# Row additions moved to TensorE, a merged scan, weights loaded in pieces and a later softplus in a Mamba block kernel

## The chip, the core and the metric

The kernel runs on one core of one Trainium2 chip. A core has five engines that run their own instruction streams in order: TensorE (PE, matrix products, with a separate row PEld for loading the stationary operand), VectorE (DVE), ScalarE (ACT), GpSimd (POOL) and SyncE (SP, which here only issues DMA transfers). The metric is the device time of one execution in microseconds (us), taken as the median of several runs. Times inside an execution come from one profiled execution and count from the start of its span.

## What is computed

The input is a tensor of 4 batches by 1024 rows by 256 columns, in fp32. The block has two halves, each around a residual sum:

```python
x = x + attn(layernorm(x))
x = x + ffn(layernorm(x))

# attn(h): a Mamba layer and a gated MLP
h = h + mamba(rmsnorm(h))
h = h + silu(rmsnorm(h) @ gate.T) * (rmsnorm(h) @ up.T) @ down.T

# mamba(u): z, x, B, C, dt_raw = split(u @ in_proj.T)
dt = softplus(dt_raw @ dt_proj.T + bias)
state = exp(dt * A) * state + (dt * x) * B      # for each of 1024 rows, one after the other
y = sum over 32 states of state * C
out = (y + x * D) * silu(z) @ out_proj.T

# ffn(x): hidden of 1024
out = fwht(silu(x @ W1.T) * (x @ W3.T)) @ W2.T
```

The state has 256 channels times 32 states for each batch, so the recurrence is 8192 independent scans over 1024 rows per batch. This scan is the heart of the kernel. The Hadamard transform (fwht) is folded into W2 at the start of the kernel (`w2h`).

## The kernel before

**Units, quarters and ticks.** The work is cut into eight units: four batches, each in two chunks of 512 rows (c = 0 and c = 1, in this order). A chunk with c = 0 starts with a zero state; its last states are kept in `carry` and are the start of the scans of the c = 1 chunk. The 8192 scans of a unit are cut into 16 groups called q, each a tile `da` of 128 partitions by 4 by 512. A group takes two ticks, each of which handles two of the four 512-column tiles. So a unit has 32 ticks, t0 to t31 in the text, and there are 128 groups in all.

**One tick of the scan** has these steps. DMA has brought dt, repeated over partitions, into `da` (`dma_da`, L753 is the common helper `spread`, from the DRAM tile `dtd`), dt times x into `ub` (`dma_ub`, from the DRAM tile `ud`), and C into `cr`. ACT turns `da` into exp(A * dt) for two tiles, two ticks ahead of their use (`exp`, L791). DVE multiplies `ub` by B (`times_b`, L819: `bx` = `ub` * `pb`, 1024 columns in PSUM, where `pb` is a copy of B made once in 16 ticks by `copy_b`, L808), and then runs two scans of 512 columns, in place in `da` (`scan`, L828). After a group POOL multiplies all 2048 columns by C (`times_c`, L841) and PE sums over states by a selecting matmul into the PSUM tile `py` (`sum_states`, L852; the first of eight groups also adds x * D by the diagonal `dd`, L850). There are five `da` buffers and four `ub` buffers.

**Around the scan** two functions put the dense work of other units into the same ticks. `pre(u, H)` makes the inputs of a unit before its first tick H: normalisation, projections, softplus (`act_dt`, L440), and the writes of dt, dt * x, B and C to DRAM. `post(u, E)` does the rest of a unit after its last tick, E being the first tick of the next unit: `y` (L870) copies `py` to `yt`; out_proj with weights `wo`; RMS norm; gate and up (`wg`, `wu`); down (`wd`); layer norm; W1 and W3; and W2 (`w2h`), which runs in the unit after that. So in a unit of the steady state, t3 has out_proj of the unit before, t5 to t8 W2 of the unit before that, t11 to t16 gate and up, t19 to t22 down, t27 to t34 W1 and W3. `many` is true for the first six units, whose `post` is spread over a whole unit.

**Adding to the residual rows.** `hr` holds the rows of a unit's normalised input; out_proj, down and W2 are added to it. `add_rows` issues the matmuls for four row tiles of 128 (L322) and has three ways to add. Way "pe": one more matmul of the identity with `hr` (L320) starts the accumulation in PSUM, and ACT (`replace`, L336) copies the sum back into `hr`. Way "pool": ACT copies the product from PSUM (`evict`, L344), and POOL adds it one tick later (L348). No way: DVE adds straight from PSUM (L332). Down uses "pe"; out_proj of the first six units and W2 of the first seven use "pool". `hr` itself is made by ACT from x (`scaled_rows`, L210) in t3 and t4 of the next unit.

**The order** is written by hand. `at(tick, lane, fn)` puts a step into a lane of a tick, and a loop runs the lanes of each tick in a fixed order: PE, ACT, `times_b`, ACTb (there `copy_b`), the exponentials, the first scan, DVE, the second scan, POOL0, `times_c`, POOL, `sum_states`, PEend, ACTend, SP, `dma_ub` for the tick four later, `dma_da` for the group three later, `dma_cr`, SPend. The `yt` copy is put into ACTend of the tick t2 while the loop is running, behind what stands there already. Each engine executes its instructions in this order; SP issues the DMAs in it, and a transfer whose source or buffer is not free holds up those behind it on SP. In unit 0, the weights `had`, `wd`, `w1` and `w3` are loaded by SP at ticks 5, 9, 15 and 21.

The lines that the steps of the prediction name: L320 and L322 the matmuls of `add_rows`, L332, L336, L344 and L348 its ways to add, L440 softplus, L791 exp, L808 the copy of B, L819 bx, L828 the scan, L841 the product with C, L850 and L852 the sums, L870 the `yt` copy, L236 projections (`project`), L280 `up` and L284 `product` of `gated`, L210 `scaled_rows`.

Of the kernel before, what the change touches and what calls it, by code (L numbers as in the profile page):

```python
# [9 lines left out]
F32 = mybir.dt.float32  # L10
AF = mybir.ActivationFunctionType
ALU = mybir.AluOpType
# [3 lines left out]
P = 128  # L16
BATCH, SEQ, DM = 4, 1024, 256
DFF = 704
HID = 1024
T = 512  # L20
# [7 lines left out]
def tile_block(ctx: ExitStack, tc: tile.TileContext, a, out):  # L28
# [20 lines left out]
    nc = tc.nc  # L49

    wp = ctx.enter_context(tc.tile_pool(name="w", bufs=1))
    p1 = ctx.enter_context(tc.tile_pool(name="p1", bufs=1))
# [5 lines left out]
    dr = ctx.enter_context(tc.tile_pool(name="dr", bufs=2, space=DRAM))  # L58
# [7 lines left out]
        return ps_m.tile([P, T], F32, tag="dense", name="dense")  # L66


    def load(name, shape, src, queue=nc.sync):
        t = wp.tile(shape, F32, tag=name, name=name)  # L70
        queue.dma_start(out=t, in_=src)
        return t
# [32 lines left out]
    W = {}  # L105
# [1 line left out]
    def load_k(name, cols, queue=nc.sync):  # L107
        W[name] = load(name, [P, 2, cols], a[name].rearrange("(k p) f -> p k f", p=P), queue)

    def load_wd():  # L110
        wd = W["wd"] = wp.tile([P, 6, DM], F32, tag="wd", name="wd")
        nc.sync.dma_start(
            out=wd[:, 0:5, :], in_=a["wd"][0:640, :].rearrange("(k p) f -> p k f", p=P)
        )
        nc.sync.dma_start(out=wd[0:64, 5, :], in_=a["wd"][640:DFF, :])

    def load_first():

# [129 lines left out]
    def at(tick, lane, fn, *args):  # L248
        todo[tick][lane].append(partial(fn, *args))

    def run(tick, lane):
        for fn in todo[tick].pop(lane, ()):
            fn()
# [109 lines left out]
    def pre(u, H):  # L363

        s = {}
# [69 lines left out]
        def act_dt(h):  # L435
            if h == 0:
                s["dt"] = [p2.tile([P, T], F32, tag="dt", name="dt") for _ in range(2)]
                u["dtd"] = dr.tile([2, 32, 4, T], F32, tag="dtd", name="dtd")
                u["ud"] = dr.tile([2, 32, 4, T], F32, tag="ud", name="ud")
            nc.scalar.activation(s["dt"][h], s["pv"][h], AF.Softplus, bias=dtb[:, h : h + 1])  # L440

        def dma_dt(h):
            nc.sync.dma_start(out=u["dtd"][h].rearrange("m b t -> b m t"), in_=s["dt"][h])

        def make_u(h, eng):
            s["du"] = p1.tile([P, T], F32, tag="du", name="du")
# [160 lines left out]
        for b in range(4):  # L607
            at(H - 19 + b, "SPend", dma_xr, 0, (b,))
            at(H - 14 + b, "SPend", dma_xr, 1, (b,))
        at(H - 15, "PE", pe_dt)  # L610
        at(H - 15, "PE", pe_c, 0)
        if H == 32:
            for h in range(2):
                at(H - 11, "PE", pe_z, h)
                at(H - 11, "ACTend", act_z, h)
        at(H - 15, "ACT", act_dt, 0)
        at(H - 15, "ACT", act_dt, 1)
        at(H - 14, "ACT", act_c, 0)
        at(H - 13, "POOL", make_u, 0, nc.gpsimd)
        at(H - 13, "SPend", dma_dt, 0)  # L620
        at(H - 11, "SPend", dma_c, 0)
        at(H - 11, "SPend", dma_u, 0)
        at(H - 10, "PE", pe_c, 1)
        at(H - 9, "ACT", act_c, 1)
        at(H - 1, "SPend", dma_c, 1)
# [5 lines left out]
    def post(u, E, other):  # L631


        s = {}
        last = u is us[-1]

        many = us.index(u) < len(us) - 2
# [34 lines left out]
        def store(lo=0, n=TT):  # L672
# [3 lines left out]
                in_=u["hr"][:, lo : lo + n, :],  # L676
            )

        at(E + 3, "ACT", hr, (0, 1))
        at(E + 4, "ACT", hr, (2, 3))  # L680
        add_rows(
            (E + 3,) * TT,
            u,
            lambda: [u["yt"][:, k, :] for k in range(2)],
            lambda: [W["wo"][:, k, :] for k in range(2)],
            "PEend",
            way="pool" if many else None,
        )
        for i in range(2):
            at(E + (5 + i if many else 4), "ACTend", row_stats, u, "hr", (2 * i, 2 * i + 1), False)  # L690
# [10 lines left out]
        for i in range(2):  # L701
# [8 lines left out]
            way="pe",  # L710
# [14 lines left out]
        for i in range(3):  # L725
# [5 lines left out]
            u,  # L731
            lambda: u["g"],
            lambda: [w2h[:, c, :] for c in range(8)],
            way=None if last else "pool",
        )
        if last:
            at(o2[1] + 1, "SPend", store, 0, 2)
# [20 lines left out]
    def dma_da(q):  # L758
        s = qs[q]
        s["da"] = pda.tile([P, 4, T], F32, tag="da", name="da")  # L760
        for b in (0, 2):
            spread(s, s["da"][:, b : b + 2, :], "dtd", b, 2)

    def dma_ub(q, half):
        s = qs[q]
        s["ub", half] = pub.tile([P, 2, T], F32, tag="ub", name="ub")
        spread(s, s["ub", half], "ud", 2 * half, 2)
# [18 lines left out]
    def exp(q, b):  # L786
        s = qs[q]
        if q == 0 and b == 0:
            s["da"] = pda.tile([P, 4, T], F32, tag="da", name="da")
        da = s["da"][:, b, :]  # L790
        nc.scalar.activation(  # L791
            da,
            da if q else s["u"]["pdt", b],
            AF.Exp,
            scale=an[:, s["h"], s["j"], b, s["g"] : s["g"] + 1],
        )

    def carry_of(s):
        return s["u"]["carry"][:, s["h"], s["j"], :, s["g"]]
# [10 lines left out]
    def times_b(q, b0):  # L810
        s = qs[q]
        u = s["u"]
        if q == 0:
            s["bx"] = ps_x.tile([P, 2, T], F32, tag="bx", name="bx")
            for i in range(2):
                nc.vector.tensor_tensor(s["bx"][:, i, :], u["pu", b0 + i], u["br", 0], ALU.mult)
            return
        s["bx"] = ps_x.tile([P, 2, T], F32, tag="bx", name="bx")
        nc.vector.tensor_tensor(  # L819
            s["bx"], s["ub", b0 // 2], u["pb"].unsqueeze(1).broadcast_to([P, 2, T]), ALU.mult  # L820
        )

    def scan(q, b):
        s = qs[q]
        u = s["u"]
        da = s["da"][:, b, :]
        start = 0.0 if u["c"] == 0 else carry_of(s)[:, b : b + 1]
        nc.vector.tensor_tensor_scan(da, da, s["bx"][:, b % 2, :], start, ALU.mult, ALU.add)  # L828

    def times_c(q, parts=(slice(0, 4),), eng=nc.gpsimd):  # L830
        s = qs[q]
        u = s["u"]
        if u["c"] == 0:
            if s["n"] == 0:
                kept = p2.tile([P, 2, 4, 4, 2], F32, tag="carry", name="carry")
                u["carry"] = us[us.index(u) + 1]["carry"] = kept
            nc.gpsimd.tensor_copy(carry_of(s), s["da"][:, :, T - 1])
        for part in parts:
            da = s["da"][:, part, :]
            n = da.shape[1]  # L840
            eng.tensor_tensor(da, da, s["cr"].unsqueeze(1).broadcast_to([P, n, T]), ALU.mult)  # L841

    def sum_states(q):
        s = qs[q]
        u = s["u"]
        first, last = s["n"] % 8 == 0, s["n"] % 8 == 7
        if first:
            u["py"] = ps_y.tile([P, T], F32, tag="y", name="py")
            x = u["xr"][:, s["h"], :]
            nc.tensor.matmul(u["py"], lhsT=dd[:, s["h"], :], rhs=x, start=True, stop=False)  # L850
        for b in range(4):
            nc.tensor.matmul(  # L852
                u["py"][32 * b : 32 * b + 32, :],
                lhsT=rsel[:, 2 * s["j"] + s["g"], :],
                rhs=s["da"][:, b, :],
                start=False,
                stop=last,
            )
        if last:
            if q == NQ - 1:  # L860
                at(2 * q + 4, "DVE", y_z_last, u)
            else:
                at(2 * q + 4, "ACTend", y, u, s["h"])
                at(2 * q + 5, "POOL0", y_z, u, s["h"])
# [14 lines left out]
    for k, u in enumerate(us):  # L879
        pre(u, 32 * k)  # L880
# [5 lines left out]
        nc.vector.tensor_scalar(nega, nega, -1.0, None, ALU.mult)  # L886

    at(-20, "PE", wake_pe)
    at(-18, "ACTend", load_first)
    at(-17, "ACTend", weights_ready)  # L890
    for h in range(2):
# [4 lines left out]
    at(-1, "SPend", dma_cr, 1)  # L896
    loads = [
        (5, load_had),
        (9, load_wd),
        (15, load_k, "w1", HID),  # L900
        (21, load_k, "w3", HID),
    ]
    for t, *f in loads:
        at(t, "SPend", *f)
# [11 lines left out]
    def has(q):  # L916
        return 0 <= q < NQ

    tick = min(todo)
    while todo:  # L920
        q, half = divmod(tick, 2)
        run(tick, "PE")
        run(tick, "ACT")
        if has(q) and tick:
            times_b(q, 2 * half)
        run(tick, "ACTb")
        if has(q + 1):
            for b in (2 * half, 2 * half + 1):
                exp(q + 1, b)
        if has(q):  # L930
            scan(q, 2 * half)
        run(tick, "DVE")
        if has(q):
            scan(q, 2 * half + 1)
        run(tick, "POOL0")
        if half == 0 and has(q - 1) and q < NQ:
            times_c(q - 1)
        elif q in (NQ - 1, NQ) and tick >= 2 * NQ - 1:

            if tick == 2 * NQ - 1:  # L940
                times_c(NQ - 1, (slice(0, 2),))
            elif tick == 2 * NQ:
                times_c(NQ - 1, (slice(2, 4),), nc.vector)
        run(tick, "POOL")
        if half == 1 and has(q - 1):
            sum_states(q - 1)
        run(tick, "PEend")
        run(tick, "ACTend")
        run(tick, "SP")
        for x in (2, 3) if tick == -1 else (tick + 4,):  # L950
            if tick >= -1 and has(x // 2):
                dma_ub(*divmod(x, 2))
        if half == 1 and has(q) and has(q + 3):
            dma_da(q + 3)
        if tick == -1:
            dma_da(2)
        if half == 1 and has(q) and has(q + 2):
            dma_cr(q + 2)
        run(tick, "SPend")
        assert not todo[tick], (tick, list(todo[tick]))  # L960
        del todo[tick]
        tick += 1
# [68 lines left out]
```

## Time and profile before

| what | us |
|---|---|
| median of 3 runs | 1137.57 (1137.0 to 1138.73) |
| profiled execution | 1138.95 |
| its span | 1137.1 |
| scan L828, 512 of 512 columns, busy | 612.6 |
| bx L819, 254, busy | 312.0 |
| product with C on POOL, L841, 128 x 4.525 | 579.2 |
| additions on POOL, L348, 26 x 1.276 | 32.9 |

The scan's number is the sum of its two rows, 314.0 with a carried start and 298.6 with zero. The profile lists busy times of each engine, groups of instructions by source line with their operands (output first, then inputs), and what ended the idle time ahead of a group. A timeline gives start and length of single instructions, with the idle time ahead of them in square brackets and what released them. PE's granted clock is in tenths of full speed; it is 0.914 on average over the span. Windows of the span give the busy time of each engine, here by unit: unit 0 takes 19.8 to 155.6, unit 1 to 279.3, unit 2 to 404.5, unit 3 to 530.2, unit 4 to 652.9, unit 5 to 779.2, unit 6 to 901.9, unit 7 to 1031.1, and the dense work of the last unit to the end. Each border is the time at which the first bx of the unit starts. Each matmul of the program has two records in the profile.

### The profile page before, as it was taken

How to read it: one execution, taken by the hardware profiler on the slowest of the kernel's cores; microseconds unless marked ns; L12 is line 12 of the kernel's file. 1: busy time of each engine (PE TensorE's matmuls, PEld its weight loads, DVE VectorE, ACT ScalarE, POOL GpSimd, SP SyncE). 2: the span in 40 equal slices, each digit the busy share in tenths (PEclk: the TensorE clock that was granted, in tenths of full speed). 3: DMA queues.
4: the chain of work that ended last, by engine and by line, in shares of the span. 5: the costliest groups of instructions: out<-in, count | busy, mean ns of one | idle time of the engine just before them, and what ended most of it. 6: DMA issues, size and time to landing. Idle time of an engine off the chain costs nothing.

```text
span 1137.1 us, 12421 instructions
## 1 busy us (share of the span) xinstructions
PE 988.5 (87%) x3470; PEld 476.0 (42%) x3470; DVE 944.5 (83%) x813; ACT 804.5 (71%) x1443; POOL 882.9 (78%) x512
## 2 busy tenths in 40 slices
PE   8565237979999899989999899989998999897998
PEld 3121003343544345443634355433634364434555
DVE  4899799999988999899998999899998989994000
ACT  3957355787969797887879787878777787584331
POOL 6766568878898899788998899888988888785222
PEclk9767557998999899989999899989999899898999
DMA  7999999989998899998999999998998979860000
GB/s 227 377 358 334 336 316 307 331 312 311 312 334 304 327 298 314 350 312 295 322 348 303 327 305 322 320 328 302 311 339 302 322 262 315 287 219 1 1 18 19
DMA packets 107748, 321.93 MB, mean 283 GB/s; under 512 B 11360, under 2 KB 22048, under 8 KB 107680
## 3 DMA queue, kind: packets, MB, share of 16 engines
q1 hardware_dynamic: 105824, 318.39, 80.8%
q10 hardware_dynamic: 1856, 2.75, 0.7%
q8 instruction: 28, 0.46, 0.2%
q14 instruction: 40, 0.33, 0.1%
HBM read 302.22 MB, written 18.87 MB: 282 GB/s over the span
## 4 chain that ended last, share of the span: by engine, by line
PE 44%; DMA 18%; ACT 13%; DVE 11%; issue 8%; POOL 4%; SPq 0%; DVEq 0%; POOLq 0%; ACTq 0%
PE dense L236 29%; DMA da<-dtd 10%; PE dense L322 9%; DVE da L828 6%; DMA ub<-ud 6%; DVE bx L819 5%; ACT da L791 5%; PE py L852 5%; POOL da L841 3%; DMA xr<-xbd 1%; ACT up L280 1%; ACT L791 1%; DMA cr<-cd 1%; ACT si L273 1%; ACT hn L210 1%
## 5 line engine op out<-in xcount | busy, mean ns | idle before, releaser
L841 POOL TENSOR_TENSOR da<-da,cr 128x2048 f32<-128x2048 f32 x128 | 579.2, 4525 | 53.5 <-DVE da L828 14.3
L791 ACT ACTIVATE da<-da,nega 128x512 f32<-128x512 f32 x508 | 335.0, 714 | 62.5 <-DMA da<-dtd 61.9
L828 DVE TENSOR_TENSOR_SCAN da<-da,carry,bx 128x512 f32<-128x512 f32 x256 | 314.0, 1268 | 24.9 <-DMA ub<-ud 5.1
L819 DVE TENSOR_TENSOR bx<-ub,pb 128x1024 f32<-128x1024 f32 x254 | 312.0, 1228 | 25.6 <-DMA ub<-ud 13.4
L828 DVE TENSOR_TENSOR_SCAN da<-da,bx 128x512 f32<-128x512 f32 x256 | 298.6, 1207 | 26.5 <-ACT da L791 8.6
L236 PE MATMUL dense<-xt,w 128*128 128x512 f32 x512 | 240.8, 624 | 4.2 <-ACT xt L230 4.2
L852 PE MATMUL py<-da,rsel 128*32 128x512 f32 x1024 | 157.3, 680 | 96.6 <-POOL da L841 96.5
L236 PEld LDWEIGHTS dense<-xt,w 128*128 128x128 f32 x512 | 99.0, 199 | 142.3 <-issue 112.8
L322 PE MATMUL dense<-w2h,g 128*128 128x256 f32 x512 | 116.1, 383 | 1.2 <-ACT ut L230 1.2
L284 POOL TENSOR_TENSOR g<-si,up 128x512 f32<-128x512 f32 x64 | 81.0, 1272 | 38.2 <-ACT up L280 38.1
L322 PEld LDWEIGHTS dense<-w2h,g 128*128 128x128 f32 x512 | 95.7, 190 | 26.3 <-issue 10.9
L852 PEld LDWEIGHTS py<-da,rsel 128*32 128x32 f32 x1024 | 23.3, 113 | 191.3 <-POOL da L841 123.3
L280 ACT COPY up<-dense 128x512 f32<-128x512 f32 x112 | 63.2, 578 | 51.7 <-PE dense L236 51.4
L322 PE MATMUL dense<-wd,m 128*128 128x256 f32 (+1 forms) x384 | 96.1, 391 | 3.8 <-POOL m L284 3.8
L236 PE MATMUL dense<-ut,win 128*128 128x512 f32 x192 | 97.3, 640 | 0.7 <-ACT ut L230 0.7
L236 PE MATMUL dense<-ht,wg 128*128 128x512 f32 x192 | 87.6, 600 | 2.4 <-ACT ht L230 2.4
L284 POOL TENSOR_TENSOR m<-si,up 128x512 f32<-128x512 f32 (+1 forms) x48 | 60.0, 1272 | 33.1 <-ACT up L280 33.1
L273 ACT ACTIVATE si<-dense 128x512 f32<-128x512 f32 x112 | 61.7, 595 | 33.7 <-PE dense L236 33.3
L322 PEld LDWEIGHTS dense<-wd,m 128*128 128x128 f32 (+1 forms) x384 | 71.1, 192 | 23.9 <-issue 10.0
L236 PE MATMUL dense<-ht,wu 128*128 128x512 f32 x160 | 73.9, 601 | 0.6 <-ACT si L273 0.4
L236 PEld LDWEIGHTS dense<-ut,win 128*128 128x128 f32 x192 | 38.2, 205 | 56.0 <-issue 52.2
L791 ACT ACT_TABLE_LOAD x46 | 59.0, 1283 | 0.8
(105 smaller groups left out, 826.2 us busy)
## 6 DMA issues: line engine op xcount, KB each, us to landing
da<-dtd SPq DMA_DIRECT2D x254, 512.0 KB
ub<-ud SPq DMA_DIRECT2D x254, 512.0 KB
cr<-cd SPq DMA_DIRECT2D x64, 256.0 KB
x<-in_x SPq DMA_DIRECT2D x8, 512.0 KB
dtd<-dt SPq DMA_DIRECT2D x16, 256.0 KB
ud<-du SPq DMA_DIRECT2D x16, 256.0 KB
cd<-cc SPq DMA_DIRECT2D x16, 256.0 KB
xr<-xbd SPq DMA_DIRECT2D x60, 64.0 KB
```

What stands on the lines that cost most here:

```text
L210: nc.scalar.activation(dst[:, t, :], src[:, t, :], AF.Identity, bias=bias[:, t : t + 1] if bias is not None else 0.0, scale=scale[:, t : t ...
L236: nc.tensor.matmul(dst[:n], lhsT=w[:, k, col : col + n], rhs=src[:, k, :], start=(k == 0), stop=(k == 1),)
L273: nc.scalar.activation(g[i]["si"][:n], g[i]["pg"][:n], AF.Silu)
L280: nc.scalar.copy(g[i]["up"][:n], g[i]["pu"][:n])
L284: nc.gpsimd.tensor_tensor(u[dst][c][:n], g[i]["si"][:n], g[i]["up"][:n], ALU.mult)
L322: nc.tensor.matmul(dst, lhsT=left[k][:, t * P : (t + 1) * P], rhs=right[k], start=(k == 0 and way != "pe"), stop=(k == n - 1),)
L791: nc.scalar.activation(da, da if q else s["u"]["pdt", b], AF.Exp, scale=an[:, s["h"], s["j"], b, s["g"] : s["g"] + 1],)
L819: nc.vector.tensor_tensor(s["bx"], s["ub", b0 // 2], u["pb"].unsqueeze(1).broadcast_to([P, 2, T]), ALU.mult)
L828: nc.vector.tensor_tensor_scan(da, da, s["bx"][:, b % 2, :], start, ALU.mult, ALU.add)
L841: eng.tensor_tensor(da, da, s["cr"].unsqueeze(1).broadcast_to([P, n, T]), ALU.mult)
L852: nc.tensor.matmul(u["py"][32 * b : 32 * b + 32, :], lhsT=rsel[:, 2 * s["j"] + s["g"], :], rhs=s["da"][:, b, :], start=False, stop=last,)
```

## The change

It has four parts.

1. For the first six units out_proj and W2 use way "pe" in `add_rows`: one identity matmul for each row tile, and ACT's copy goes to `hr`. The first half of `hr` is now made in ACTend of t2, the second in ACT of t3, one tick earlier each. W2 of the seventh unit stays on POOL.
2. In c = 0 units the two scans of a tick become one scan over 1024 columns. So that the second tile starts from zero, the first column of each tile of `da` is zero: `dtd` is now one DRAM tile for each c, of which the c = 0 one gets a zero column at the start (`zero_columns`), and the writes of dt leave that column out. The very first `da` is cleared by a memset, and its exponentials leave the column out as well. In c = 1 units there are two scans as before; the lane DVE comes after both.
3. The dt projection moves from t17 to the end of t19, softplus from t17 to the end of t20, the product dt * x from t19 to t21, and the writes of `dtd` and `ud` from t19 and t21 to t20 and t22.
4. `wd` is loaded in three pieces at ticks 7, 9 and 11, `w1` and `w3` in quarters of 256 KB at ticks 14, 16, 18, 20 and 22, 24, 26, 28.

```diff
+    dtds = [dr.tile([2, 32, 4, T], F32, tag=f"dtd{i}", name="dtd") for i in range(2)]
+
+    def zero_columns():
+        zero = p1.tile([P, 2], F32, tag="zero", name="zero")
+        nc.vector.memset(zero, 0.0)
+        nc.scalar.dma_start(out=dtds[0][:, :, :, 0].rearrange("h m b -> (m b) h"), in_=zero)
...
+    def load_quarter(name, i):
+        if i == 0:
+            W[name] = wp.tile([P, 2, HID], F32, tag=name, name=name)
+        k, cols = i // 2, slice(i % 2 * T, (i % 2 + 1) * T)
+        nc.sync.dma_start(out=W[name][:, k, cols], in_=a[name][k * P : (k + 1) * P, cols])
...
-                u["dtd"] = dr.tile([2, 32, 4, T], F32, tag="dtd", name="dtd")
+                u["dtd"] = dtds[u["c"]]
...
         def dma_dt(h):
-            nc.sync.dma_start(out=u["dtd"][h].rearrange("m b t -> b m t"), in_=s["dt"][h])
+            rows = u["dtd"][h].rearrange("m b t -> b m t")
+            lo = int(u["c"] == 0)
+            nc.sync.dma_start(out=rows[:, :, lo:], in_=s["dt"][h][:, lo:])
...
-        at(H - 15, "PE", pe_dt)
+        at(H - 13, "PEend", pe_dt)
         at(H - 15, "PE", pe_c, 0)
...
-        at(H - 15, "ACT", act_dt, 0)
-        at(H - 15, "ACT", act_dt, 1)
+        at(H - 12, "ACTend", act_dt, 0)
+        at(H - 12, "ACTend", act_dt, 1)
         at(H - 14, "ACT", act_c, 0)
-        at(H - 13, "POOL", make_u, 0, nc.gpsimd)
-        at(H - 13, "SPend", dma_dt, 0)
+        at(H - 11, "POOL", make_u, 0, nc.gpsimd)
+        at(H - 12, "SPend", dma_dt, 0)
         at(H - 11, "SPend", dma_c, 0)
-        at(H - 11, "SPend", dma_u, 0)
+        at(H - 10, "SPend", dma_u, 0)
...
-        at(E + 3, "ACT", hr, (0, 1))
-        at(E + 4, "ACT", hr, (2, 3))
+        for i in range(2):
+            at(E + (2 if many else 3) + i, "ACTend" if many and i == 0 else "ACT", hr, (2 * i, 2 * i + 1))
...
             "PEend",
-            way="pool" if many else None,
+            way="pe" if many else None,
         )
...
             lambda: [w2h[:, c, :] for c in range(8)],
-            way=None if last else "pool",
+            way="pe" if many else None if last else "pool",
         )
...
     def scan(q, b):
         s = qs[q]
         u = s["u"]
-        da = s["da"][:, b, :]
-        start = 0.0 if u["c"] == 0 else carry_of(s)[:, b : b + 1]
-        nc.vector.tensor_tensor_scan(da, da, s["bx"][:, b % 2, :], start, ALU.mult, ALU.add)
+        if u["c"] == 0:
+            da = s["da"][:, b : b + 2, :].rearrange("p b t -> p (b t)")
+            bx = s["bx"].rearrange("p b t -> p (b t)")
+            nc.vector.tensor_tensor_scan(da, da, bx, 0.0, ALU.mult, ALU.add)
+            return
+        for i in range(2):
+            da = s["da"][:, b + i, :]
+            start = carry_of(s)[:, b + i : b + i + 1]
+            nc.vector.tensor_tensor_scan(da, da, s["bx"][:, i, :], start, ALU.mult, ALU.add)
...
     loads = [
         (5, load_had),
-        (9, load_wd),
-        (15, load_k, "w1", HID),
-        (21, load_k, "w3", HID),
+        *((7 + k, load_wd, k) for k in (0, 2, 4)),
+        *((14 + 2 * i, load_quarter, "w1", i) for i in range(4)),
+        *((22 + 2 * i, load_quarter, "w3", i) for i in range(4)),
     ]
...
             scan(q, 2 * half)
         run(tick, "DVE")
-        if has(q):
-            scan(q, 2 * half + 1)
```

More of the change, by code (lines that the diff above doesn't have):

```diff
@@ L108, in load_k, with load_wd @@
         W[name] = load(name, [P, 2, cols], a[name].rearrange("(k p) f -> p k f", p=P), queue)
[L110 to L115, printed above, removed]
+    def load_wd(k):
+        if k == 0:
+            W["wd"] = wp.tile([P, 6, DM], F32, tag="wd", name="wd")
+        wd = W["wd"]
+        if k == 4:
+            nc.sync.dma_start(out=wd[:, 4, :], in_=a["wd"][512:640, :])
+            nc.sync.dma_start(out=wd[0:64, 5, :], in_=a["wd"][640:DFF, :])
+        else:
+            src = a["wd"][k * P : (k + 2) * P, :].rearrange("(k p) f -> p k f", p=P)
+            nc.sync.dma_start(out=wd[:, k : k + 2, :], in_=src)
+    def load_quarter(name, i):
[3 more added lines that the diff above has]
+        nc.sync.dma_start(out=W[name][:, k, cols], in_=a[name][k * P : (k + 1) * P, cols])
     def load_first():
@@ L789, in exp @@
             s["da"] = pda.tile([P, 4, T], F32, tag="da", name="da")
-        da = s["da"][:, b, :]
+        lo = int(s["u"]["c"] == 0)
+        if q == 0 and b == 0:
+            nc.vector.memset(s["da"][:, :, 0], 0.0)
+        da = s["da"][:, b, lo:]
         nc.scalar.activation(
             da,
-            da if q else s["u"]["pdt", b],
+            da if q else s["u"]["pdt", b][:, lo:],
             AF.Exp,
@@ L825, in scan @@
         u = s["u"]
-        da = s["da"][:, b, :]
-        start = 0.0 if u["c"] == 0 else carry_of(s)[:, b : b + 1]
-        nc.vector.tensor_tensor_scan(da, da, s["bx"][:, b % 2, :], start, ALU.mult, ALU.add)
+        if u["c"] == 0:
[7 more added lines that the diff above has]
+            nc.vector.tensor_tensor_scan(da, da, s["bx"][:, i, :], start, ALU.mult, ALU.add)
     def times_c(q, parts=(slice(0, 4),), eng=nc.gpsimd):
@@ L888, in tile_block @@
     at(-20, "PE", wake_pe)
+    at(-19, "ACTend", zero_columns)
     at(-18, "ACTend", load_first)
```

## The prediction

> **What bounds the kernel now.** I read the busy shares first, then the work by unit, then the rows of one unit. A unit is 512 rows of a batch and 32 ticks; I call them t0 to t31. In its windows I put the borders where the first bx of a unit starts.
>
> The page's shares, and busy time of each engine in the windows of units 1, 4 and 5:
>
> ```profile
> PE 988.5 (87%) x3470; PEld 476.0 (42%) x3470; DVE 944.5 (83%) x813; ACT 804.5 (71%) x1443; POOL 882.9 (78%) x512
> ```
> ```profile
> core 0: us, PE busy (x) PEld busy (x) DVE busy (x) ACT busy (x) POOL busy (x), PEclk, DMA share, GB/s
> ...
> 155.60:279.30 123.70, 98.42 (x325) 42.55 (x326) 117.75 (x97) 89.88 (x168) 98.64 (x47) 0.83 0.92 316
> ...
> 530.20:652.90 122.70, 115.23 (x423) 56.26 (x423) 113.94 (x97) 101.14 (x185) 110.07 (x68) 0.96 0.93 322
> 652.90:779.20 126.30, 119.53 (x435) 57.92 (x434) 117.73 (x96) 101.38 (x185) 108.97 (x55) 0.96 0.91 316
> ```
>
> Unit 1 has the same DVE work as unit 5 and 21 us less of PE: only DVE bounds it (32 ticks of 3.87 us). From unit 2 on PE has 115 to 120 us of work in 123 to 126: two engines are nearly full, and which one is waited for changes within a unit. VectorE's rows around t15 to t19 of unit 4 show the handover, ScalarE's show why:
>
> ```profile
> 586.53 1.23 DVE L819 TENSOR_TENSOR bx<-ub,pb 128x1024 f32<-128x1024 f32 x1
> 587.85 2.33 DVE L828 TENSOR_TENSOR_SCAN da<-da,bx 128x512 f32<-128x512 f32 x2
> 590.46 1.23 DVE L819 TENSOR_TENSOR bx<-ub,pb 128x1024 f32<-128x1024 f32 x1 [0.27 <-ACT pb L808]
> ...
> 605.45 2.33 DVE L828 TENSOR_TENSOR_SCAN da<-da,bx 128x512 f32<-128x512 f32 x2 [2.46 <-ACT da L791]
> ```
> ```profile
> 588.12 0.59 ACT L280 COPY up<-dense 128x512 f32<-128x512 f32 x1 [2.20 <-PE dense L236]
> 588.60 1.34 ACT L791 ACTIVATE da<-da,nega 128x512 f32<-128x512 f32 x2
> 589.84 0.58 ACT L808 COPY pb<-br 128x512 f32<-128x512 f32 x1
> ...
> 602.12 1.27 ACT L440 ACTIVATE dt<-dense,dtb 128x512 f32<-128x512 f32 x2
> 603.40 1.28 ACT L791 ACT_TABLE_LOAD   x1
> 604.70 1.34 ACT L791 ACTIVATE da<-da,nega 128x512 f32<-128x512 f32 x2
> ```
>
> The bx of t16 needs pb, which ScalarE copies behind an up that waited 2.20 us for PE. pb ends at 590.42, bx starts at 590.46. T15 to T16 takes 3.93 us against 3.69 for the tick before, so PE's work from out_proj (t3) to the up products (t14) has no slack left: **what is added to PE there reaches DVE one for one**. At t19 softplus with its two table loads delays the exponentials, and DVE stands 2.46 us. Elsewhere in the unit DVE is back to back. How PE enters this stretch, and where it has spare time:
>
> ```profile
> 543.57 0.56 ACT L870 COPY yt<-py 128x512 f32<-128x512 f32 x1
> ...
> 545.50 1.10 ACT L210 ACTIVATE hr<-x,s 128x256 f32<-128x256 f32 x2
> ```
> ```profile
> 544.19 1.12 PE L850 MATMUL py<-xr,dd 128*128 128x512 f32 x2 [0.95 <-ACT yt L870]
> ...
> 610.31 0.70 PE L320 MATMUL dense<-hr,ident 128*128 128x256 f32 x2
> ...
> 627.72 2.04 PE L852 MATMUL py<-da,rsel 128*32 128x512 f32 x8 [3.39 <-POOL da L841]
> ```
>
> PE waits 0.95 us for the yt copy, and 3.39 us at t24 for GpSimd. After that gap the granted clock reads 0.5 for 10.24 us (627.85 to 638.09); the same in units 2, 3, 5 and 6. Gaps of 2.3 us and more were followed by it, of 1.5 us and less not. Unit 0 differs: its DVE waits for ub six times, 13.4 us in all, the longest wait right behind the load of w3:
>
> ```profile
> 133.16 1.23 DVE L819 TENSOR_TENSOR bx<-ub,pb 128x1024 f32<-128x1024 f32 x1 [5.77 <-DMA ub<-ud]
> ```
>
> **The change, part by part.**
>
> **Adds on TensorE.** GpSimd loses 24 adds of 1.276 us, 30.6 us in all. That is worth nothing by itself: from t3 to t16 neither PE nor the scan's inputs wait for these adds, and the gap at t24 waits for GpSimd's product of scan results, which follows DVE. PE gains one ident pair for each row tile: 4 at t3 and one each at t5 to t8, eight in a full unit. The same pair is in the trace (matmul of 256 columns, two records): 603.88 to 604.42, 610.31 to 610.85, 613.72 to 614.26, 619.95 to 620.39, so 0.44 to 0.54 us, and 3.5 to 4.3 us a unit. I take 3.9. ScalarE's eviction is the same copy with another target, zero. But hr(0,1) moves ahead of the yt copy: two scalings of about 0.5 us (1.10 for the pair in the row above), on which PE's 0.95 wait already ends. PE starts 1.0 us later. Together **+4.9 us before t16** in units 2 to 6. Unit 1 has only out_proj's half (1.8 + 1.0) and 21 us of free PE: zero. Unit 7 gets only W2's half: +1.8.
>
> **Softplus later.** pe_dt leaves t17 for the end of t19, softplus for the end of t20, dtd, the product u and ud follow by one or two ticks. At t19 the exponentials no longer stand behind it: 2.4 us less in units 2, 4, 6, 1.8 in 3 and 5 (their stalls are 1.7 and 2.0). What is late next: at t20 the block of two table loads and two softplus (1.28 + 1.27 + 1.28 = about 3.9 us) stands ahead of the exponentials of t21 and t22, whose results have 2.15 to 4.5 us of slack at t20 to t22 now, and 2.4 more once t19 is gone. I count no new stall; the bound is the present 2.4 again. SP at the end of t20 waits for softplus with the ub of t25 queued behind it, about 1.5 us; ub has 3 us and more of slack there, zero. ud now goes behind ub(26), which landed 0.66 us too late in unit 4: a gain of at most that.
>
> **One scan for two tiles.** A pair takes 2.331 us now: 1.221 + 1.194 with the second starting 84 ns before the first ends. The trace has no scan of 1024. [...] I take 0.043, [...]. By the row 128 scans save 5.5 us of DVE time, of which only t16 to t31 of units 2, 4, 6 are on the path (before t16 PE paces, unit 0 is paced by DMA): 15 x 0.043 = 0.65 a unit. The merged scan waits for both exponentials, 0.6 us less slack; the least is now 1.83 outside t19. The zero column costs a memset and a small DMA at the start, beside the loading of x, and one fewer column in the writes: zero.
>
> **Weights in pieces.** At unit 0's longest wait, 0.75 MB net of weights and the ud write move from ahead of ub(26) to behind it. DMAs land there 1.27 us per 512 KB, so 1.9 us, and ud took 2.1 to 2.5: 4.4. But the same bytes still come, and unit 0 is full of DMA (share 0.94): between -1 and -5.5, I take **-4**. wd and w1 in pieces: only the order within the same bytes, zero.
>
> **Sum.** Units 2, 4, 6: 4.9 - 2.4 - 0.65 = +1.85 each, +5.6. Units 3, 5: 4.9 - 1.8 = +3.1, less what a smaller t24 gap gives. PE comes to t24 about 4 later and DVE about 2.5, so the gap shrinks from 3.4 to about 2, at the edge of the halved clock. These units' way from t31 to yt is 19.25 us against 17.26 in unit 4, which bounds the gain by about 1.8; I take half: +2.2 each, +4.4. Unit 7: +1.8 less up to 3 from the better clock before it, -1. Unit 0 -4, units 1 and the 106 us tail behind the last scan 0. Together +5.0. The profiled execution took 1138.95 us (span 1137.1 and 1.85 around it); it becomes 1144. It lies 1.4 above the median, so the median goes from 1137.57 to **1142.5**.
>
> **Rivals.** *Faster: the clock stays full.* Place: the t24 gap in units 2 to 6. PE loses up to half of 10.24 us of work each time. If the later PE keeps the gap under the 1.5 us that did no harm, PE enters t3 of the five next units (3 to 7) earlier; of the 5.1 us lost at most I let half arrive: 12.5 less, of which 4.6 is in the sum already (0.9 + 0.9 + 2.8): 1142.5 - 8 = about 1134.5 (1132 to 1137). For it: the added work itself fills the gap. Against: in unit 4 yt waits for the chain of scan, GpSimd's product and py, not for earlier PE work. *Much slower: PE holds the da buffers.* The load of da(q+3) reuses the buffer that PE's py(q-2) read, and SP issues in order, so ub and cr stand behind it. DMA latency is 9 to 11 us. Where py runs over 3 us later against the scan than now (ub's slack), each further us is a stall; 2 to 3 us in five units: +10 to +14, about 1153. For it: t3 puts four more pairs ahead of the next py. Against: da has five buffers. [...]
>
> **How the numbers follow.** Forecast 0.48 (own range 1139 to 1147, from pairs of 3.5 to 4.3, unit 0 of -1 to -5.5, the clock's 0 to 1.8), clock 0.30, buffers 0.17, fast scan 0.05. What a measurement can tell from no change is 0.2%, 2.3 us. Faster: 0.23 of the clock's, 0.05 of the scan's = 0.28. Same: 0.07 of the clock's, 0.10 of the forecast = 0.17. Slower: 0.38 + 0.17 = 0.55. The range 1132 to 1151 leaves out the fast scan and most of the buffers' case, some 0.2.
>
> **What would show it.** T15 to T16 of units 2 to 6 grows from 3.9 to about 8 us (or stalls spread over t12 to t16); no stall of 2 us at t19, nor at t20 to t22; PE's wait for yt near 2 us; scans of 1024 at 2.29 us; unit 0's ub waits near 9 us in all; unit 1 unchanged. Wrong if T16 stays at 3.9 (PE had slack that I don't see), or if the 0.5 rows are gone and units 3, 5, 7 are shorter.

## The result

| | us |
|---|---|
| before, median | 1137.28 (1136.62 to 1138.73, 4 runs) |
| changed, median | 1156.39 (1153.53 to 1158.62, 4 runs) |
| ratio | 1.0165, 95% interval 1.0138 to 1.0191 |
| profiled execution of the changed kernel, span | 1157.54, 1155.8 |

The change costs 19 us, where the forecast had 5.

The page of the changed kernel, its busy shares and two groups that are new or grown:

```profile
PE 1000.4 (87%) x3566; PEld 491.5 (43%) x3566; DVE 938.2 (81%) x687; ACT 804.8 (70%) x1443; POOL 854.5 (74%) x488
...
L856 DVE TENSOR_TENSOR_SCAN da<-da,bx 128x1024 f32<-128x1024 f32 x128 | 292.7, 2287 | 32.7 <-ACT da L816 14.3
```
```profile
L339 PE MATMUL dense<-hr,ident 128*128 128x256 f32 x160 | 53.0, 413 | 1.2 <-ACT ut L249 1.2
```

GpSimd has 28 us less, VectorE 6 us less, and TensorE's busy time has grown by only 12. Busy totals say nothing of 19 us. The merged scan takes 2.287 us; the prediction named 2.29, an estimate of mine, since no row of before shows a scan of 1024. The lengths of the units (from the first bx of one to that of the next; unit 7 to the end of its last scan) show where the time is:

| | start | unit 0 | 1 | 2 | 3 | 4 | 5 | 6 | 7 | tail |
|---|---|---|---|---|---|---|---|---|---|---|
| before | 19.9 | 135.7 | 123.7 | 125.3 | 125.6 | 122.7 | 126.4 | 122.7 | 129.1 | 106.1 |
| changed | 21.8 | 131.6 | 124.0 | 125.2 | 131.1 | 125.2 | 131.6 | 126.6 | 132.8 | 106.0 |
| difference | +1.9 | -4.1 | +0.3 | -0.1 | +5.4 | +2.5 | +5.2 | +3.9 | +3.7 | 0 |
| forecast | 0 | -4 | 0 | +1.85 | +2.2 | +1.85 | +2.2 | +1.85 | -1 | 0 |

Units 2 and 4 came within 2 us of the forecast. Units 3, 5 and 6 lie 2 to 3 us above it, unit 7 4.7. VectorE's rows in unit 4 answer to those shown of before, t15 to t19:

```profile
591.45 1.23 DVE L844 TENSOR_TENSOR bx<-ub,pb 128x1024 f32<-128x1024 f32 x1
593.78 2.29 DVE L856 TENSOR_TENSOR_SCAN da<-da,bx 128x1024 f32<-128x1024 f32 x1 [1.11 <-ACT da L816]
599.19 1.23 DVE L844 TENSOR_TENSOR bx<-ub,pb 128x1024 f32<-128x1024 f32 x1 [3.12 <-ACT pb L833]
...
610.36 1.23 DVE L844 TENSOR_TENSOR bx<-ub,pb 128x1024 f32<-128x1024 f32 x1
611.68 2.29 DVE L856 TENSOR_TENSOR_SCAN da<-da,bx 128x1024 f32<-128x1024 f32 x1
```

T15 to T16 is 7.74 us instead of 3.93, and the stall at t19 is gone. Both are as forecast. (Only in unit 2 T15 to T16 was 6.14 us before already, with a wait for pb, and this unit grew least.) VectorE did save what was expected in t16 to t31: 62.41 us before, 59.59 now in unit 4. The next three fences are of the changed kernel, too: ScalarE and TensorE at t3, TensorE at t24, and the waits of TensorE in all.

```profile
547.93 1.08 ACT L229 ACTIVATE hr<-x,s 128x256 f32<-128x256 f32 x2
548.91 0.56 ACT L903 COPY yt<-py 128x512 f32<-128x512 f32 x1
```
```profile
549.52 1.13 PE L883 MATMUL py<-xr,dd 128*128 128x512 f32 x2 [1.35 <-ACT yt L903]
...
632.05 1.06 PE L885 MATMUL py<-da,rsel 128*32 128x512 f32 x8
633.74 1.06 PE L885 MATMUL py<-da,rsel 128*32 128x512 f32 x8 [0.62 <-POOL da L874]
638.08 2.81 PE L242 MATMUL dense<-ident,hn 128*128 128x128 f32 x8 [3.28 <-ACT hn L229]
```
```profile
PE dense L242 <- ACT hn L229: 13.6, 7, 3.3
```

Of the kernel before, the same two lines:

```profile
630.34 2.81 PE L223 MATMUL dense<-ident,hn 128*128 128x128 f32 x8 [0.58 <-ACT hn L210]
```
```profile
PE dense L223 <- ACT hn L210: 4.7, 7, 1.1
```

The gap at t24 did shrink, from 3.39 to 0.62 us. Right behind it stands a wait that was 0.58 us in unit 4 before: the transposes of hn, 3.28 us (in all 13.6 us in seven times; 4.7 before). hn follows the last down product through a copy into hr, the row statistics, GpSimd's small steps and a scaling. From down's end at 632.1 to the transposes at 638.08 this takes 6 us, in which TensorE has only the two rows of sums to do. ScalarE works through it without a pause, with four exponentials in between:

```profile
632.16 0.59 ACT L355 COPY hr<-dense 128x512 f32<-128x512 f32 x1 [1.19 <-PE dense L341]
...
635.00 2.54 ACT L816 ACTIVATE da<-da,nega 128x511 f32<-128x511 f32 x4
637.44 2.06 ACT L229 ACTIVATE hn<-hr,s 128x256 f32<-128x256 f32 x4
```

GpSimd's small steps (635.18 to 637.08) lie beside these exponentials, so the 5.96 us are ScalarE's own. Before, the small steps stood behind one of GpSimd's products, hn waited for them, and the way took 7.0 us in this unit:

```profile
629.68 2.08 ACT L210 ACTIVATE hn<-hr,s 128x256 f32<-128x256 f32 x4 [0.92 <-POOL s L656]
```

So TensorE's gap was not filled, it changed its name, and the clock still halves behind it:

```profile
core 0: us, PE busy (x) PEld busy (x) DVE busy (x) ACT busy (x) POOL busy (x), PEclk, DMA share, GB/s
628.00:638.00 10.00, 6.18 (x33) 2.97 (x31) 9.35 (x7) 8.69 (x21) 7.45 (x9) 0.93 0.89 318
638.00:648.00 10.00, 8.62 (x16) 3.85 (x16) 9.58 (x6) 6.99 (x13) 9.21 (x11) 0.56 1.01 392
```

The columns are the window, its length, busy time by engine with the number of instructions, and then the granted clock: 0.56 in the ten us behind the gap.

This led to **theory L**: from unit 2 on the period is TensorE's own loop, with its waits for ScalarE in it. I cut it at the diagonal matmul (dd) that opens the sums at t3, the end of the last down product, and the first transpose of hn. Means over the four periods from unit 2 to unit 6:

| | dd to down's end | to hn | to next dd | dd to dd |
|---|---|---|---|---|
| before | 79.15 | 7.25 | 37.96 | 124.35 |
| changed | 82.51 | 5.97 | 40.13 | 128.60 |

The first part grew by 3.4 us, eight identity pairs of 0.42 us, one for one. **Theory D** is the prediction's: TensorE sets the pace from t3 to t16, VectorE from t16 to t31, so what VectorE saves there comes off.

### The profile page after: what moved, and what is told of

Read it like the earlier page. It is cut to its first block, busy times and chain, and to the rows that moved or that the text cites. A ratio compares the mean times of both kernels' runs of the same rounds, so it can differ in the third digit from the quotient of the medians.

```text
span 1155.8 us, 12343 instructions
## 1 busy us (share of the span) xinstructions
PE 1000.4 (87%) x3566; PEld 491.5 (43%) x3566; DVE 938.2 (81%) x687; ACT 804.8 (70%) x1443; POOL 854.5 (74%) x488
## 4 chain that ended last, share of the span: by engine, by line
PE 53%; ACT 11%; DMA 10%; POOL 4%; issue 2%; DVE 1%; SPq 0%; POOLq 0%; ACTq 0%; DVEq 0%
PE dense L255 29%; PE dense L341 15%; DMA da<-dtd 8%; PE py L885 5%; ACT da L816 4%; PE dense L339 3%; POOL da L874 2%; POOL m L303 1%; ACT up L299 1%; ACT L816 1%; DMA ub<-ud 1%; DMA out<-hr 1%; ACT si L292 1%; PE py L883 1%; ACT junk L199 0%
## 5 line engine op out<-in xcount | busy, mean ns | idle before, releaser
L816 ACT ACTIVATE da<-da,nega 128x511 f32<-128x511 f32 (+1 forms) x508 | 335.3, 714 | 72.0 <-DMA da<-dtd 66.7
L856 DVE TENSOR_TENSOR_SCAN da<-da,bx 128x1024 f32<-128x1024 f32 x128 | 292.7, 2287 | 32.7 <-ACT da L816 14.3
L885 PE MATMUL py<-da,rsel 128*32 128x512 f32 x1024 | 152.6, 667 | 85.6 <-POOL da L874 85.6
L255 PE MATMUL dense<-ut,win 128*128 128x512 f32 x192 | 94.5, 624 | 2.9 <-ACT ut L249 2.9
L355 ACT COPY hr<-dense 128x512 f32<-128x512 f32 x39 | 22.3, 591 | 59.7 <-PE dense L341 59.7
```

The costliest lines, as they stand in the source:

```text
L255: nc.tensor.matmul(dst[:n], lhsT=w[:, k, col : col + n], rhs=src[:, k, :], start=(k == 0), stop=(k == 1),)
L816: nc.scalar.activation(da, da if q else s["u"]["pdt", b][:, lo:], AF.Exp, scale=an[:, s["h"], s["j"], b, s["g"] : s["g"] + 1],)
L856: nc.vector.tensor_tensor_scan(da, da, bx, 0.0, ALU.mult, ALU.add)
L885: nc.tensor.matmul(u["py"][32 * b : 32 * b + 32, :], lhsT=rsel[:, 2 * s["j"] + s["g"], :], rhs=s["da"][:, b, :], start=False, stop=last,)
```

## The experiments

Ratios stand against runs of the kernel before on the same chip, with their 95% interval. Differences in us are those of the medians; lengths of units and dd to dd come from one profiled execution of each kernel.

**1. The parts apart.** Four kernels.

The change without its additions on TensorE:

```diff
-            way="pe" if many else None,
+            way="pool" if many else None,
...
-            way="pe" if many else None if last else "pool",
+            way=None if last else "pool",
```

(and `hr` in ACT of t3 and t4 again).

> The change without its additions on TensorE (these and hr are as before; merged scan, later softplus and pieces stay). Theory L (from unit 2 on the period of a unit is TensorE's own loop, from one out_proj to the next; VectorE's savings there are worth nothing): start +2.0, unit 0 -4.1, units 1 to 7 as before, so about 1135 us. Theory D (the prediction's: TensorE sets the pace from t3 to t16, VectorE from t16 to t31): a further 2.4 x 3 + 1.8 x 2 + 0.65 x 3 = 12.8 us less, about 1122 us.

Measured 1131.03 us, ratio 0.9936 (0.9917 to 0.9955): 4 us below theory L and 9 above theory D.

The reverse of it, the kernel before with these edits alone:

> The kernel before with the additions on TensorE and the earlier hr alone. Theory L: what units 2 to 7 lost, 19.1 - 2.0 + 4.1 = +21 us: 1158 us, dd to dd longer by about 4.2 us (3.45 of identity pairs, the rest hr ahead of yt). Theory D: +4.9 in five units and +1.8 in unit 7, +26: 1163 us.

Measured 1160.03 us, ratio 1.0187 (1.0172 to 1.0202), 22 us more, between the two theories; dd to dd 128.88 on average. The way to down's end is as in the changed kernel: 82.60 us.

Softplus later, alone:

```diff
-        at(H - 15, "PE", pe_dt)
+        at(H - 13, "PEend", pe_dt)
...
-        at(H - 15, "ACT", act_dt, 0)
-        at(H - 15, "ACT", act_dt, 1)
+        at(H - 12, "ACTend", act_dt, 0)
+        at(H - 12, "ACTend", act_dt, 1)
...
-        at(H - 11, "SPend", dma_u, 0)
+        at(H - 10, "SPend", dma_u, 0)
```

> The kernel before with the later softplus alone. Theory L: the stall of VectorE at t19 goes, and the time with it does not: dd to dd stays within 1 us, 1135 to 1138 us (unit 0 may gain 2 from ud behind ub). Theory D: 2.4 x 3 + 1.8 x 2 = 10.8 less, about 1126 us.

Measured 1132.70 us, ratio 0.9943 (0.9926 to 0.9961): 5 us less, between the two theories. By units: unit 0 4.4 us shorter with w3 still whole, units 2 to 6 together 5.2 shorter, unit 7 2.3 longer. TensorE in unit 4 of this kernel, at t24:

```profile
620.93 1.16 PE L852 MATMUL py<-da,rsel 128*32 128x512 f32 x8 [0.94 <-POOL da L841]
624.95 0.33 PE L223 MATMUL dense<-ident,hn 128*128 128x128 f32 x1 [2.86 <-ACT hn L210]
```

The same exchange as in the changed kernel, with no added matmul: less waiting for GpSimd's product, more for hn. Down's end to hn fell from 7.25 to 5.97, and 0.7 of the 1.3 us was given back on the way to the next dd.

The merged scan alone:

```diff
+        if u["c"] == 0:
+            da = s["da"][:, b : b + 2, :].rearrange("p b t -> p (b t)")
+            bx = s["bx"].rearrange("p b t -> p (b t)")
+            nc.vector.tensor_tensor_scan(da, da, bx, 0.0, ALU.mult, ALU.add)
+            return
```

> The kernel before with the merged scan and what it needs (zero column) alone. Theory L: +2.0 at the start and nothing else: 1139 us. Theory D: +2.0 at the start and 0.65 x 3 less: 1137 us. If the start's 2.0 came from elsewhere, unit 0 starts at 19.8 as before.

Measured 1139.42 us, ratio 1.0017 (1.0005 to 1.0028). No gain from 128 merged scans; the small loss fits a later start (20.7 us, 19.9 before).

The first two runs bear on the main point. With the additions, everything else in the change is worth 1160.0 - 1156.4 = 3.6 us by the medians (2.5 by the ratios, whose intervals overlap), and unit 0 alone gained 4.1. In units 2 to 7 the kernel with the additions alone takes 773.6 us and the whole change 772.4: **the 12.8 us that VectorE was to save in t16 to t31 are worth about 1 us** once TensorE has the added work. Without it they are worth 3 us (748.6 us for these units, 751.8 before).

**2. Pieces, hr, and work for TensorE at t22.** The weights in pieces alone:

> The kernel before with the weights in pieces alone. The prediction (w3 behind ub(26) shortens unit 0's longest wait): unit 0 1 to 2 us shorter, about 1136. Theory after the run with softplus alone (there unit 0 was 4.4 us shorter with w3 still whole, so the write of ud behind ub(26) is what unit 0 gains by): unit 0 within 1 us, no change of the time.

Measured 1134.83 us, ratio 0.9978 (0.9967 to 0.9989), unit 0 3.2 us shorter. My second theory falls: the pieces do help by themselves. So does softplus with the later ud (4.4), and the two together give 4.1 in the changed kernel. These lengths cannot show whether the two gains add, since the five kernels with neither spread from 133.4 to 135.8 us. The wait for ub(26) can: it is 5.5 to 5.8 us in those five, 4.4 with the later ud, 3.5 with the pieces, and 1.5 to 2.3 in the seven kernels with both. There the gains add.

The changed kernel with hr behind the yt copy:

```diff
-        for i in range(2):
-            at(E + (2 if many else 3) + i, "ACTend" if many and i == 0 else "ACT", hr, (2 * i, 2 * i + 1))
+        at(E + 3, "ACT", hr, (0, 1))
+        at(E + (3 if many else 4), "ACT", hr, (2, 3))
```

> The changed kernel with hr(0,1) and hr(2,3) behind the yt copy, in ACT of t3. If hr ahead of yt delays TensorE's start by 1.0 us and that counts one for one (theory L): dd to dd 0.8 to 1.0 us shorter in units 2 to 6, 1151 to 1152 us. If only the identity pairs count: 1156.

Measured 1149.76 us, ratio 1.0120 (1.0099 to 1.0141), dd to dd 127.06 on average: 1.5 less than in the changed kernel, 6.6 us in all by the medians (5 by the ratios). dd's wait for yt falls from 1.37 to 0.38 us on average, the 1.0 us of the two scalings; besides, the clock was halved for 6.8 us instead of 10.2 in two of the four periods. The place of two scalings on ScalarE is worth about a third of the loss.

The kernel before with more work for TensorE at t22:

```diff
             s["pc"] = project(win, CC + h * P, P, u["ut"])
+            if h and u is not us[0]:
+                project(win, CC + h * P, P, u["ut"], s["pc"])
```

> The kernel before with the projection of C's second half at t22 done twice (1.77 us of TensorE work per unit, into the same PSUM tile; the output is the same), in a place where the prediction saw TensorE off the path. Theory L: it comes ahead of the last down product, so dd to dd grows by 0.8 to 1.8 us in units 2 to 6: 1141 to 1146 us. Theory D: the 3.4 us gap at t24 swallows it: 1137 us.

Measured 1139.00 us, ratio 1.0015 (0.9999 to 1.0031): a miss for L, whose lower end was 1141. The trace has down's end 1.72 us later, and then down's end to hn at 5.97 instead of 7.25. The gap had some 1.3 us of room before ScalarE's chain to hn binds (the same 5.97 as in the changed kernel and with softplus later). So in the kernel before TensorE is not alone on the path.

Both projections of C (3.6 us a unit) behind down, in the kernel without the additions:

```diff
-        at(H - 15, "PE", pe_c, 0)
+        at(H - 9, "PE", pe_c, 0)
...
-        at(H - 10, "PE", pe_c, 1)
+        at(H - 9, "PE", pe_c, 1)
```

(with their copies at H - 8 and the write of the first at H - 7).

> The change without its additions on TensorE, and with both projections of C (1.8 us each, at t17 and t22) behind the last down product, in the gap where TensorE waits. Theory L: down ends 3.6 us earlier, the gap ahead of the transposes of hn is filled, dd to dd falls until VectorE's own pace is reached (119.6 and 124.0 us): about 10 us less than the 1131 of the run without the additions, 1119 to 1125. Theory D: 1131.

Measured 1135.57 us, ratio 0.9971 (0.9945 to 0.9998), single runs from 1127.0 to 1140.2: a miss. TensorE in unit 4 and in unit 6 of its profile says why:

```profile
607.59 1.94 PE L885 MATMUL py<-da,rsel 128*32 128x512 f32 x8 [2.51 <-POOL da L874]
609.46 3.78 PE L450 MATMUL dense<-raw,dtw 128*128 128x512 f32 x4
```
```profile
857.16 1.07 PE L885 MATMUL py<-da,rsel 128*32 128x512 f32 x8 [2.51 <-POOL da L874]
858.16 1.98 PE L450 MATMUL dense<-raw,dtw 128*128 128x512 f32 x4
```

With less to do after t16 TensorE waits for GpSimd at t20 already, ahead of three of the four row tiles of down. In unit 4 the clock halves at this wait (the same four matmuls take 3.78 us), in unit 6 it does not (1.98). The granted clock of the ten us from the start of each wait:

```profile
core 0: us, PE busy (x) PEld busy (x) DVE busy (x) ACT busy (x) POOL busy (x), PEclk, DMA share, GB/s
605.10:615.10 10.00, 7.51 (x21) 3.57 (x22) 9.35 (x7) 7.14 (x15) 9.84 (x7) 0.66 0.74 240
854.70:864.70 10.00, 7.54 (x33) 4.67 (x34) 8.99 (x7) 7.62 (x13) 9.84 (x7) 1.00 0.84 279
```

Moving work later moved the gap earlier.

**3. More work for VectorE, and less before down.** The doubled bx asks about the failed step alone. In the changed kernel bx is computed twice in two ticks:

```diff
             times_b(q, 2 * half)
+            if 2 <= q // 16 <= 6 and tick % 32 in (28, 30):
+                u = qs[q]["u"]
+                nc.vector.tensor_tensor(
+                    qs[q]["bx"], qs[q]["ub", half],
+                    u["pb"].unsqueeze(1).broadcast_to([P, 2, T]), ALU.mult
+                )
```

> The changed kernel with bx done twice in t28 and t30 of units 2 to 6: 2.46 us more for VectorE in each of five units, 12.3 in all, in the stretch that the prediction called VectorE's (the output is the same). Theory L: TensorE is behind the scans there, so the sum py comes when TensorE gets to it: 0 to +3 us on the changed kernel's 1156. Theory D: +12.3, about 1169.

Measured 1159.50 us, ratio 1.0187 (1.0155 to 1.0220), 2.5 us (by the ratios) to 3.1 us (by the medians) above the changed kernel. The two intervals overlap; together they leave room for nothing to about 7 of the 12.3 us. VectorE did the work, in unit 4:

```profile
641.56 1.23 DVE L844 TENSOR_TENSOR bx<-ub,pb 128x1024 f32<-128x1024 f32 x1
642.83 1.23 DVE L962 TENSOR_TENSOR bx<-ub,pb 128x1024 f32<-128x1024 f32 x1
```

In this profile, of the fastest of the four runs, dd to dd is 128.63, to 0.03 us that of the changed kernel. VectorE comes later to the end of a unit, and dd comes earlier after the start of the next (17.68 us in unit 5, 19.59 before the doubling). Theory D falls for the changed kernel.

The same edit in the kernel before:

> The kernel before with bx done twice in t28 and t30 of units 2 to 6 (12.3 us more for VectorE; the output is the same). It asks whether the failed step was wrong for the kernel before already. Theory D: +12.3, about 1149.5. Theory L alone: 0 to +3. Both engines near balance (at t31 TensorE's sums end 7.8 us behind the tick in unit 4, which leaves room, and 5.3 in unit 5, which leaves none): 2.5 in units 3 and 5, little in 2, 4 and 6: +4 to +7, about 1143.

Measured 1144.47 us, ratio 1.0062 (1.0038 to 1.0087): 7 (by the ratios) to 8 us of 12.3, by its interval 4 to 10. dd to dd is 125.3 in the periods from the c = 0 units 2 and 4 and 127.3 in those from the c = 1 units 3 and 5, against 124.07 to 124.80 before: the doubling counts little where there was room and in full where there was none. So before the change the two engines are near balance, and VectorE's time counts for about 0.6 of itself; after it, for about a quarter or less.

Without the additions, the second projection of C alone behind down (`pe_c, 1` at H - 9, its copy at H - 8):

> The change without its additions on TensorE, and with the second projection of C alone (1.8 us, t22) behind the last down product. The first one stays at t17, so TensorE comes to t20 no earlier. Theory L: dd to dd 1 to 1.8 us shorter in units 2 to 6, 5 to 9 us less than 1131: 1122 to 1126. Theory D: 1131.

Measured 1130.42 us, ratio 0.9935 (0.9911 to 0.9959), within 0.6 us of the kernel without that move. Down ends 1.7 us earlier as meant, hn 0.5 to 1.4 us later behind it, and dd to dd falls only from 124.17 to 123.21. VectorE's own pace (119.6 and 124.0 us, an estimate: twice what it takes for t16 to t31 in c = 0 and c = 1 units; mean 121.8) is near by then, so another 1.8 us of TensorE has no place to go. A miss for L as the only limit.

The same with two scans for each tick:

> As the run before it in this call, but with two scans for each tick as in the kernel before (no zero column): pieces, later softplus and the second projection of C behind down. Theory L: within 2 us of that run, since VectorE's 0.04 us per pair are not waited for. Theory D: 2 us more in units 2, 4 and 6.

Measured 1129.98 us, ratio 0.9924 (0.9904 to 0.9944). The merged scan adds nothing that these runs can tell. This version, softplus later, weights in pieces and one projection moved, with additions on GpSimd and two scans, is faster than both kernels: 7.5 us below the kernel before on its chip.

## Why the prediction was wrong

**The step that failed** is in the sum: "Units 2, 4, 6: 4.9 - 2.4 - 0.65" and "Units 3, 5: 4.9 - 1.8 = +3.1, less what a smaller t24 gap gives". It puts TensorE's work before t16 and VectorE's after t16 in series and subtracts the one engine's gains from the other's cost. They are two loops side by side, closed over the units: the longer one sets the period, and the other waits for it at some place, here at yt and at pb. VectorE's being back to back from t16 to t31 was read as its being the limit there. But the next dd comes when TensorE has worked off W1 and W3; in the changed kernel its sums at t31 of unit 4 end 10.4 us behind the tick, 7.8 before. The saved 2.8 us of unit 4 came back as a dd that lay 3.5 us later in unit 5 (19.59 us after the unit's start, 16.12 before). Of 12.8 us about 1 was kept.

VectorE's own times show the same in all units. Sums over units 2 to 6 against the kernel before, in us, split where the bx of t16 starts:

| | t0 to t15 | t16 to t31 | together |
|---|---|---|---|
| forecast, without the clock's 1.8 | +24.5 | -12.8 | +11.8 |
| changed | +28.4 | -11.5 | +16.9 |
| additions and hr alone | +20.7 | +0.7 | +21.4 |
| changed without the additions | +4.9 | -10.9 | -6.0 |
| changed, bx twice | +19.4 | +0.2 | +19.6 |
| before, bx twice | -0.3 | +10.3 | +10.0 |

The saving in t16 to t31 came, 11.5 of 12.8 us. But t0 to t15 then took 7.7 us more than with the additions alone (28.4 and 20.7), and unit 7 another 3.3. The doubled bx is the reverse: 11.7 us more in t16 to t31, 9.0 less in t0 to t15. In the kernel before, the 10 us of the doubled bx stay in these units; its run is only 7 to 8 us longer, with unit 0 2.3 us and unit 7 1.0 us shorter in the profile.

Point by point:

- Identity pairs: right. 3.4 us a unit, 0.42 each, just under the low end of the bound (3.5).
- hr ahead of yt: right. I had 1.0 us a unit, and dd's wait for yt differs by 1.0 between hr ahead and hr behind. That wait is 1.37 us and not near 2, since with hr behind yt it is 0.38 in the changed kernel, and no longer the 0.95 that unit 4 had before. Additions and hr together, summed at 26.3 us, measured 22 alone and 25 on top of the rest (1156.4 - 1131.0).
- Stall at t19: it went, and in units 2 to 6 no new one came at t20 to t22, as said. Unit 7 got one (below). Its worth was wrong: forecast 10.8 us, about 3 by itself (5.2 less in units 2 to 6, 2.3 more in unit 7), nothing with the additions.
- Merged scan: the saving of 43 ns a pair was an estimate of mine that no row of before showed. Measured it is 44 ns (2.331 us for two scans, 2.287 for one). Forecast 1.95 us on the path, measured none.
- The clock: the second wrong term, -4.6 us in units 3, 5 and 7. The gap at t24 shrank (forecast about 2 us; 0.62 in unit 4, 1.99 in unit 5), but I named no next wait. It was hn's, 3.28 and 1.82 us, and the clock halved there as before (in unit 3 at t24 already, behind 1.98 us), for 10.2 us in units 2 to 5 and 6.8 in unit 6. The reading that gaps of 1.5 us and less do no harm was weak too: the gap of 1.48 us before (unit 1) lay in a stretch that was halved already, and the longest without harm at full clock was 1.25.
- Unit 0: -4 forecast, -4.1 measured. The wait for ub(26) fell by 3.6 us, 4.4 forecast. That the length agrees to 0.1 is luck, since it varies by 2 to 3 us between kernels that are alike in it.
- Zero column: forecast at nothing. Unit 0 starts 1.9 us later here; over the seven profiled kernels with it the start is 20.98 us on average, 19.81 over the seven without, so some 1.2 us.
- GpSimd's 30.6 us: said to be worth nothing. No run takes them away by themselves, so this is not shown.

**Unit 7** was forecast at -1 and grew by 3.7. No gain of clock came, and one wait makes 3.3 us of it: at t20 VectorE waits 4.10 us for exponentials (0.76 before). On ScalarE they stand behind a copy of down's rows, which waits for TensorE (of the changed kernel, ScalarE and VectorE):

```profile
1000.91 0.59 ACT L355 COPY hr<-dense 128x512 f32<-128x512 f32 x1 [3.66 <-PE dense L341]
```
```profile
1004.49 2.45 DVE L861 TENSOR_TENSOR_SCAN da<-da,carry,bx 128x512 f32<-128x512 f32 x2 [4.10 <-ACT da L816]
```

TensorE comes there 3.7 us later after the start of the unit than before: its dd starts 1.2 us later, W2 has four identity pairs (1.7 us at 0.42 each), and in down the clock is halved for 6.8 us instead of 3.4. This fits theory L: what VectorE had gained waits here for TensorE at the last.

Of the rivals, that of the full clock did not come, though it named the right place, the gap at t24. The one with the da buffers came near in size (1153) by chance; it has no support: the waits of bx for ub in the changed kernel are 8.3 us in all, every one in unit 0. The fast scan, given 0.05 as a guess at how short a scan of 1024 could be, did not come: 2.287 us against the pair's 2.331.

**What stays open:** the way from hn to the next dd grew by 2.2 us. The runs put about 1.1 on the additions with hr and 0.7 to 1.2 on the later softplus. In the traces 0.7 of it is dd's wait for yt (0.66 before, 1.37 now on average) and 0.6 the wait of the first W1 product for xt (0.52 and 1.10), both copied by ScalarE; the rest was not found. No run moves ScalarE's four exponentials from the way to hn, or GpSimd's small steps, by themselves.

## What to carry to other kernels

Where two engines are both nearly full in a repeating period (here, before, TensorE 94 to 95% and VectorE 93% of units 4 and 5), don't add up what one gains and the other loses: write the period of each engine's loop, take the larger, and ask of each gain in which loop it lies. Near balance neither loop alone is right: in the kernel before a part of each engine's time counted. The cheapest test is to double a piece of work on the engine that is thought to be the limit; the share of it that shows in the time (here about 0.6 before the change, about a quarter or less after it) is what a saving there is worth. And a wait that is to shrink has a second one behind it: look for what the next instruction needs and when that is ready, before counting the gap as filled.

## What the runs showed of the hardware

- A TensorE wait of 2.51 us at the same place, with the same instructions ahead of it, was met with a halved clock in one unit and not in another of the same execution (four matmuls in 3.78 and in 1.98 us, granted clock 0.66 and 1.00). In this execution 1.45 us ahead of hn in unit 5 had it behind it (0.66 over ten us), 1.57 us in unit 1 had not (1.00). So the length of the wait alone does not decide. That kernel's twelve runs spread over 13 us, those of the other eleven kernels (4 to 20 runs each) over 2 to 7.
- Two scans of 512 columns in a row, each from zero, took 2.331 us, and one of 1024 took 2.287. In the pair 84 ns of the second scan lay under the end of the first (1.221 and 1.194 us by themselves). From the means of one scan, 1.207 us for 512 columns and 2.287 for 1024, I estimate 2.1 ns a column and about 0.13 us besides; no other length was run.
- One small transfer of 256 pieces of 4 bytes, issued by ScalarE ahead of its weight loads, goes with a start that is about 1.2 us later. In the traces its issue waits for VectorE's memset (6.31 us in the changed kernel), the weight loads are issued later (9.80 instead of 8.83), and ScalarE's first copy stands behind them (13.12 instead of 11.18). It was not tried by itself.
